# Gathers of selected rows issued one by one over four blocks, with the swap of the choice, two scan steps, the last statistics and a pooling moved in a block loop

## The chip, the cores and the metric

One core of one Trainium2 chip. The metric is the device time of an execution in microseconds (us), with the median of several runs as the kernel's time. Besides, one execution was taken with the hardware profiler; its span, waits and instruction times are what "the profile" and "the trace" mean below. PE is the matmul engine (PEld its weight loads), DVE the vector engine, ACT the scalar (activation) engine, POOL the GpSimd engine, SP the queue that issues most DMAs.

## The reference, cut to what matters

Two layers over `x` of shape (4, 128, 64, 64), that is four samples (b = 0 to 3) of 4096 tokens with 128 channels. All is fp32.

```python
# layer 0: three 1x1 convolutions with PReLU, then attention over all 4096 tokens
score = softmax(einsum('nci,ncj->nij', e1, e2), axis=2)
x = x + einsum('nij,ncj->nci', score, asm)
t = to_tokens(x)                                  # (4, 4096, 128)

# layer 1, attention with a running maximum and running sums over the tokens (8 heads)
kv = silu(einsum('btd,ed->bte', ln(t), W_kv))     # k and v
s = einsum('hd,bthd->bth', q_proj, k)
m = cummax(s, axis=1)
w = cumsum(exp(s - m)[..., None] * v, axis=1)
u = cumsum(exp(s - m), axis=1)
t = t + (w / u[..., None]).mean(axis=2)

# layer 1, experts (64) choose tokens
probs = softmax(ln(t) @ gate_w.T + gate_b, axis=1)   # over the tokens
topv, topi = top_k(probs, 8)                         # 8 tokens for each expert and sample
pooled = einsum('bked,bke->bed', gather(ln(t), topi), topv)
h = gelu(pooled @ weight1); out = h @ weight2        # with bias rows
t = t + scatter_add(topi, out * topv)
```

## The kernel before

Three stages follow each other on the core. Stage one (up to about 1526 us) is layer 0: PE computes scores (`sc`, L1812), ACT their exponentials, PE the weighted sums (`av`, L1837), DVE the row sums. Stage two is a loop over blocks of 512 tokens, 8 blocks for each sample, 32 in all. Stage three is the experts and the final stores.

The block loop is a hand-written schedule: PE, ACT, DVE and POOL take their instructions in the order in which the program records them[...]. `loop` runs over `n` from 6 to 37. In one round it computes the keys of block `n` (`keys`, PE `f_pk`, ACT silu, DVE product and reduction) and values, totals, products and outputs of block `m = n - 6` (`value`: PE `f_pv`, ACT silu into `f_amb`; `totals`: `f_pt`; `products` and `outputs`: `f_po`). "Block m" below is the round of that m.

A round has named places at which other work is put in. `slot(1)` to `slot(4)` each call `point()`, which advances a counter and runs what `later(delay, fn)` has put off to it; then they run what `make_plan` has put at that place of that block with `at(block, place, fn, ...)`. Besides the slots there are "D", "T" and "G", which only run planned work: D after the first products, T after the totals are closed, G at the end of the round behind the outputs. In order of a round: keys 0 and 1, slot 1, values 0 and 1, slot 2, keys 2 and 3, first totals and products, D, slot 3, values 2 and 3, the token transpose `f_ltr` (L965) of block n + 1, slot 4, late totals, `close_totals` (DVE copy L1168), T, `weights(m + 1)` on POOL (L1092 to L1113), late products, `outputs` (PE L1185), `gate_stats`, G.

The running maximum and sum go in groups of four blocks. `keys` puts off `scan0(g)`, which starts a chain: `scan0` (PE transpose `f_str` L1026, DVE copy L1027 and scan L1028), then `scan1` (PE `f_mr` L991 and small DVE steps), `scan2`, `scan2b`, `scan3`, `scan4`. A group's last key stands in slot 2's work of block 4g - 3.

Several small results share one PSUM buffer, tag "sm" with a single copy: `f_str`, `f_mc`, `f_etr`, the gate's logits `f_pl` (L1280), the swap `f_pw` (L1309), `f_pq` and `f_pp` (L1401). Each new one waits until DVE has read the one before it.

The choice of tokens for sample b follows six blocks after the sample's last: `merge_half`, `merge_halves` (the swap: PE `f_pw`, DVE L1310 to L1315), `candidate_rows` (DVE L1321, L1323 makes the row numbers `f_at`), `exps` on ACT, `gathers` (POOL, eight indirect DMAs L1329, each of 128 rows of 512 bytes from the table in HBM into `f_e1b`), `count`, `denominators`, `select` and `pool` (PE `f_pp`, eight products with the gathered rows, DVE copy L1402).

Statistics of layer 1's first normalisation are kept per sample. Those of the last sample (b = 3) are closed in block 6 by `close_stats` (ACT square root L260, DVE L263 and L264):

```python
slot(4)
if m == 6:
    close_stats(B - 1)
```

Of the kernel before, what the change touches and what calls it, by code (L numbers as in the profile page):

```python
# [9 lines left out]
AF = mybir.ActivationFunctionType  # L10
ALU = mybir.AluOpType
# [6 lines left out]
def conv_attn_hybrid_kernel(  # L18
# [24 lines left out]
    nc = tc.nc  # L43
    B, C, N = x.shape
# [19 lines left out]
    eps5 = const.tile([P, 1], F32, tag="eps5", name="eps5")  # L64
# [763 lines left out]
    def fast():  # L828
# [14 lines left out]
        NB = len(blocks)  # L843
# [3 lines left out]
        def later(delay, fn):  # L847
            env.tasks.append((env.now + delay, fn))
# [119 lines left out]
        def keys(n, c):  # L968
            g = n // GB
            s = scan_at(g % 2).rearrange("p (i h) -> p i h", h=NH)  # L970
            pk = ps.tile([P, 2, BLK], F32, tag="kv", name=f"f_pk_{n}_{c}", bufs=2)
            for i in range(2):
                nc.tensor.matmul(  # L973
                    pk[:, i, :], xt_at(n)[:, bass.ts(c, P)], env.wks[:, bass.ts(i, BLK)],
                    start=True, stop=True,
                )
            flat = env.e1a[:, bass.ts(env.ks_count % 2, HD)]
            env.ks_count += 1
            ks = flat.rearrange("p (h c) -> p h c", h=NH)
            nc.scalar.activation(flat, pk.rearrange("p i x -> p (i x)"), AF.Silu)  # L980
            nc.vector.tensor_mul(ks, ks, env.qb)  # L981
            nc.vector.tensor_reduce(s[:, (n % GB) * CPB + c, :], ks, AX.X, ALU.add)  # L982
            if n % GB == GB - 1 and c == CPB - 1:
                later(3, lambda: scan0(g))

        def sm(what, *shape):
            return ps.tile([P, *shape] if shape else [P, P], F32, tag="sm", name=what)
# [35 lines left out]
        def scan0(g):  # L1023
            group[g] = {}
            pt = sm(f"f_str_{g}")
            nc.tensor.transpose(pt, scan_at(g % 2), ident)  # L1026
            nc.vector.tensor_copy(scan_at(SS), pt)  # L1027
            nc.vector.tensor_tensor_scan(  # L1028
                out=scan_at(MM), data0=scan_at(SS), data1=scan_at(SS), op0=ALU.max,
                op1=ALU.max, initial=LOWEST,  # L1030
            )
            later(1, lambda: scan1(g))

        def scan1(g):
            group[g]["m"] = link_rows(g, ends_to_row(g, scan_at(MM), MR, "mr"), 0, ML)
            later(2, lambda: scan2(g))
# [287 lines left out]
                out=at, in0=ci, scalar1=env.base[:, b : b + 1], scalar2=None, op0=ALU.add  # L1324
            )

        def gathers(b):
            for k in range(8):
                nc.gpsimd.indirect_dma_start(  # L1329
                    out=g_at(k), out_offset=None, in_=table[b],  # L1330
                    in_offset=bass.IndirectOffsetOnAxis(ap=sel[b]["at"][:, k : k + 1], axis=0),
                )
# [216 lines left out]
        slots = []  # L1549
# [124 lines left out]
        def layer0(env):  # L1674
            ps, one, big = env.ps, env.one, env.big
            with ExitStack() as l0:
# [286 lines left out]
                keys(LAG, 1)  # L1963
                point()

        plan = {}

        def at(i, slot, fn, *args):
            plan.setdefault((i, slot), []).append((fn, args))
# [5 lines left out]
        def make_plan():  # L1975
            turned = {}
            for lo in range(0, NB - 8, 4):
                at(lo + 4, 4, gate_root, lo, 4)
                at(lo + 5, 1, gate_close, lo, 4)
                for m in range(lo, min(lo + 4, NB - 10)):  # L1980
                    turned[m] = m + 5
            for m, i in turned.items():
                at(i, "D", gate_norm, m)
                at(i + 1, 1, gate_turn, m)
                at(i + 1, 3, gate_logits, m)
            at(NB - 4, "D", gate_root, NB - 8, 4)
            at(NB - 4, 4, gate_close, NB - 8, 4)
            at(NB - 2, "D", gate_root, NB - 4, 2)
            at(NB - 2, 4, gate_close, NB - 4, 2)
            at(NB - 1, 1, gate_root, NB - 2, 1)  # L1990
            at(NB - 1, 1, gate_close, NB - 2, 1)
            last = B - 2
            at(NB - 3, "G", exps, last, 0)
            at(NB - 3, "G", exps, last, 1)
            for m in range(NB - 10, NB - 2):
                i = NB - 5 + (m - NB + 10) // 2
                at(i, "D" if m == NB - 6 else "G", gate_norm, m)
                at(i + 1, 1 + m % 2, gate_turn, m)
                at(i + 1, (2 if i == NB - 2 else 3) + m % 2, gate_logits, m)
            at(NB - 1, 2, gate_norm, NB - 2)  # L2000
            at(NB - 1, 3, gate_turn, NB - 2)
            at(NB - 1, 4, gate_logits, NB - 2)
            for b in range(B - 2):
                i = (b + 1) * NBLK + 6
                at(i - 1, 3, merge_half, b, NBLK)
                at(i, 1, merge_halves, b)
                at(i, 3, candidate_rows, b, NBLK)
                at(i, 4, exps, b, 0)
                at(i, "G", gathers, b)
                at(i + 4, 4, exps, b, 1)  # L2010
                j = i + 5 if b + 3 == B else i + 6
                at(j, 3 if b + 3 < B else 2, count, b)
                at(j + 1, 1, denominators, b)
                at(j + 1, 3 if b + 3 < B else "G", select, b)
                at(j + 1, 4, pool, b)
            at(NB - 4, 4, merge_half, last, NBLK)
            at(NB - 3, 1, merge_halves, last)
            at(NB - 3, 2, candidate_rows, last, NBLK)
            at(NB - 3, "G", gathers, last)
            at(NB - 2, 2, count, last)  # L2020
            at(NB - 2, "G", select, last)
            at(NB - 1, 1, denominators, last)
            at(NB - 1, 4, pool, last)
            at(NB - 1, 4, merge_half, B - 1, NBLK - 1)
            at(NB - 1, "T", merge_halves, B - 1)
            at(NB - 1, "T", candidate_rows, B - 1, NBLK - 1)
            at(NB - 1, "T", gathers, B - 1)

        def loop():
            make_plan()  # L2030
            normals(LAG + 1)
            for n in range(LAG, NB + LAG):
                m = n - LAG

                def slot(p):
                    if n > LAG or p > 1:
                        point()
                    run(m, p)

                if n > LAG and n < NB:  # L2040
                    keys(n, 0)
                    keys(n, 1)
                slot(1)
                if m:
                    weigh_rows(m)
                value(m, 0)
                value(m, 1)
                slot(2)
                if n < NB:
                    keys(n, 2)  # L2050
                    keys(n, 3)
                else:
                    value(m, 2)
                open_block(m)
                totals(0)
                if n < NB:
                    totals(1)
                    products(m, 0)
                run(m, "D")
                if 2 <= m < 6:  # L2060
                    for i in range(CPB):
                        tile_stats(env.rest, B - 1, (m - 2) * NBLK + i)
                slot(3)
                if n < NB:
                    value(m, 2)
                value(m, 3)
                if n + 1 < NB:
                    tokens(n + 1)
                if n + 2 < NB:
                    normals(n + 2)  # L2070
                slot(4)
                if m == 6:
                    close_stats(B - 1)
                if n >= NB:
                    totals(1)
                    products(m, 0)
                totals(2)
                totals(3)
                close_totals(m)
                run(m, "T")  # L2080
                if m + 1 < NB:
                    weights(m + 1)
                for x4 in range(1, CPB):
                    products(m, x4)
                outputs(m)
                gate_stats(m)
                if 2 <= m < 6:
                    for i in range(CPB, 2 * CPB):
                        tile_stats(env.rest, B - 1, (m - 2) * NBLK + i)
                run(m, "G")  # L2090
                if n == NB - 1:
                    for room in (env.wks, env.held[:, bass.ts(2, HD)], slot_of(env.e1a, 0),
                                 slot_of(env.e1a, 1)):
                        load_into(room)
                if n == NB + 2:
                    load_into(slot_of(env.e1a, 2))
                if n == NB + LAG - 2:
                    load_into(slot_of(env.e1a, 3))
            while env.tasks:
                point()  # L2100
            assert not plan, plan.keys()
# [99 lines left out]
```

## Time and profile before

| | us |
|---|---|
| median of 3 runs | 2364.94 |
| lowest, highest | 2362.34, 2367.75 |
| the profiled execution, whole | 2383.13 |
| its span | 2381.1 |
| busy in the span: PE, DVE, ACT, POOL | 2271.9, 1450.8, 1095.0, 180.2 |
| PE's mean granted clock | 0.989 |

The profile was taken in another execution than the timed runs. Each part of a page is read by itself: the first gives an engine's busy time, the 40 slices show where in the span it is spent, the list of waits names who waited for whom with total, count and longest in us, and a timeline line has the start, the duration, engine, source line, operation, output and inputs, and in brackets the engine's idle time before it with what ended it. The block loop is the slices 26 to 38 of the 40:

```profile
PE   7999999999999999999999999999999999899877
PEclk9999999999999999999999999999999999999799
DMA  2000010000010000010000000102111112134394
```

### The profile page before, as it was taken

How to read it: one execution, taken by the hardware profiler on the slowest of the kernel's cores; microseconds unless marked ns; L12 is line 12 of the kernel's file. 1: busy time of each engine (PE TensorE's matmuls, PEld its weight loads, DVE VectorE, ACT ScalarE, POOL GpSimd, SP SyncE). 2: the span in 40 equal slices, each digit the busy share in tenths (PEclk: the TensorE clock that was granted, in tenths of full speed). 3: DMA queues.
4: the chain of work that ended last, by engine and by line, in shares of the span. 5: the costliest groups of instructions: out<-in, count | busy, mean ns of one | idle time of the engine just before them, and what ended most of it. 6: DMA issues, size and time to landing. Idle time of an engine off the chain costs nothing.

```text
span 2381.1 us, 43376 instructions
## 1 busy us (share of the span) xinstructions
PE 2271.9 (95%) x18530; PEld 1189.0 (50%) x18530; DVE 1450.8 (61%) x2345; ACT 1095.0 (46%) x1329; POOL 180.2 (8%) x340
## 2 busy tenths in 40 slices
PE   7999999999999999999999999999999999899877
PEld 3544444444444444444444444555555556566554
DVE  7666566556566556556555566577676668665414
ACT  2343333433333433334444544455565566456531
POOL 0000000000000000000000000112112221223200
PEclk9999999999999999999999999999999999999799
DMA  2000010000010000010000000102111112134394
GB/s 86 20 12 16 9 44 16 9 8 16 9 43 17 8 8 16 9 35 12 9 5 5 5 5 5 50 26 58 45 39 59 48 49 56 33 114 107 134 344 189
DMA packets 72587, 105.82 MB, mean 44 GB/s; under 512 B 8512, under 2 KB 44352, under 8 KB 72384
## 3 DMA queue, kind: packets, MB, share of 16 engines
q1 hardware_dynamic: 70784, 99.81, 13.4%
q8 instruction: 147, 2.41, 0.4%
q0 software_dynamic: 1024, 2.10, 0.3%
q10 hardware_dynamic: 576, 1.05, 0.1%
q14 instruction: 56, 0.46, 0.1%
HBM read 79.60 MB, written 17.04 MB: 41 GB/s over the span
## 4 chain that ended last, share of the span: by engine, by line
PE 86%; DVE 6%; ACT 4%; issue 2%; DMA 1%; another core or an unknown queue 1%; POOL 0%; SPq 0%; ACTq 0%; DVEq 0%; POOLq 0%
PE av L1837 36%; PE sc L1812 18%; PE f_pv L1128 9%; PE f_pk L973 7%; PE f_pt L1151 3%; PE f_po L1174 2%; PE pd L1863 1%; ACT f_e1a L980 1%; PE pa L1785 1%; DVE f_e1a L981 1%; PE pe L1759 1%; DVE f_e1a L982 1%; PE f_po L1185 1%; PE f_eo L1625 1%; PE f_pl L1280 1%
## 5 line engine op out<-in xcount | busy, mean ns | idle before, releaser
L1837 PE MATMUL av<-pr,am 64*128 64x512 f32 x4096 | 976.3, 591 | 1.7 <-ACT pr L1817 1.7
L1817 ACT ACTIVATE pr<-sc 128x1024 f32<-128x1024 f32 x512 | 523.6, 1023 | 779.7 <-PE sc L1812 766.8
L1824 DVE TENSOR_TENSOR acc<-acc,pr 128x1024 f32<-128x1024 f32 x480 | 586.6, 1222 | 483.9 <-ACT pr L1817 479.6
L1837 PEld LDWEIGHTS av<-pr,am 64*128 64x128 f32 x4096 | 401.3, 187 | 471.0 <-issue 457.8
L1812 PE MATMUL sc<-e,e 64*128 64x512 f32 x2048 | 534.5, 591 | 4.8 <-DMA e<-side 4.8
L1812 PEld LDWEIGHTS sc<-e,e 64*128 64x128 f32 x2048 | 201.3, 187 | 236.3 <-issue 228.6
L1128 PE MATMUL f_pv<-f_held,f_ama 128*32 128x256 f32 x4096 | 244.7, 385 | 7.7 <-ACT f_e1a L980 4.0
L973 PE MATMUL f_pk<-f_held,f_ama 128*128 128x512 f32 x512 | 240.7, 615 | 9.0 <-ACT f_amb L1133 8.5
L1133 ACT ACTIVATE f_amb<-f_pv 128x1024 f32<-128x1024 f32 x128 | 130.8, 1023 | 157.1 <-PE f_pv L1128 136.6
L981 DVE TENSOR_TENSOR f_e1a<-f_e1a,f_held 128x1024 f32<-128x1024 f32 x128 | 156.2, 1221 | 68.6 <-ACT f_e1a L980 68.3
L980 ACT ACTIVATE f_e1a<-f_pk 128x1024 f32<-128x1024 f32 x128 | 129.9, 1024 | 126.3 <-PE f_pk L973 62.6
L1128 PEld LDWEIGHTS f_pv<-f_held,f_ama 128*32 128x32 f32 x4096 | 131.5, 111 | 105.9 <-issue 20.4
L982 DVE TENSOR_REDUCE f_e1a<-f_e1a 128x8 f32<-128x1024 f32 x128 | 155.3, 1218 | 3.5
L973 PEld LDWEIGHTS f_pk<-f_held,f_ama 128*128 128x128 f32 x512 | 94.1, 193 | 122.0 <-issue 103.1
L1092 POOL COPY f_held<-f_e1a 32x32 f32<-32x32 f32 x128 | 30.3, 237 | 944.7 <-DVE f_e1a L1074 564.2
L1151 PE MATMUL f_pt<-f_amb,f_held 128*32 128x128 f32 x1920 | 83.7, 277 | 1.2 <-ACT f_amb L1133 1.2
L918 POOL MEMSET f_held<- 128x1024 f32 x1 | 1.0, 956 | 1034.8 <-DVE xn L1750 1034.8
L1151 PEld LDWEIGHTS f_pt<-f_amb,f_held 128*32 128x32 f32 x1920 | 60.2, 109 | 11.0 <-issue 5.1
L1190 DVE TENSOR_TENSOR t<-t,f_po 128x512 f32<-128x512 f32 x32 | 22.0, 687 | 56.4 <-PE f_po L1185 56.4
L956 ACT ACTIVATE f_xl<-t,ln_nb,ln_rs 128x128 f32<-128x128 f32 x128 | 52.8, 491 | 0.8 <-PE pa L1785 0.8
L1261 ACT ACTIVATE f_x<-t,f_gnb,f_grs 128x128 f32<-128x128 f32 x126 | 51.3, 482 | 0.4 <-DVE f_gnb L1242 0.4
L1821 DVE COPY acc<-pr 128x1024 f32<-128x1024 f32 x32 | 22.2, 693 | 39.3 <-ACT pr L1817 39.3
(265 smaller groups left out, 1829.2 us busy)
## 6 DMA issues: line engine op xcount, KB each, us to landing
f_e2a<-f_rd SPq DMA_DIRECT2D x128, 128.0 KB
xr<-in_xtok_dram SPq DMA_DIRECT2D x32, 256.0 KB
out_dram<-t SPq DMA_DIRECT2D x16, 512.0 KB
f_table<-f_x SPq DMA_DIRECT2D x62, 128.0 KB
f_held<-in_fw_dram SPq DMA_DIRECT2D x14, 512.0 KB
f_e1a<-in_fw_dram SPq DMA_DIRECT2D x13, 512.0 KB
x<-in_x_dram SPq DMA_DIRECT2D x12, 512.0 KB
f_amb<-in_fw_dram SPq DMA_DIRECT2D x12, 512.0 KB
```

The source lines that it names most:

```text
L956: nc.scalar.activation(xl[:, c, :], t[:, b * NCH + i, :], AF.Identity, bias=ln_nb[:, b, i : i + 1], scale=ln_rs[:, b, i : i + 1],)
L973: nc.tensor.matmul(pk[:, i, :], xt_at(n)[:, bass.ts(c, P)], env.wks[:, bass.ts(i, BLK)], start=True, stop=True,)
L980: nc.scalar.activation(flat, pk.rearrange("p i x -> p (i x)"), AF.Silu)
L981: nc.vector.tensor_mul(ks, ks, env.qb)
L982: nc.vector.tensor_reduce(s[:, (n % GB) * CPB + c, :], ks, AX.X, ALU.add)
L1128: nc.tensor.matmul(pv[a * CH : (a + 1) * CH, i, :], xt_at(m)[:, bass.ts(c * NA + i, CH)], env.wvs[:, bass.ts(a, HH * C)], start=True, stop ...
L1133: nc.scalar.activation(env.amb[:, bass.ts(c, HD)], pv.rearrange("p i x -> p (i x)"), AF.Silu)
L1151: nc.tensor.matmul(env.pt[i * CH : (i + 1) * CH, :], lhs, rhs, start=i not in env.begun, stop=False, skip_group_check=True,)
L1812: nc.tensor.matmul(sc[:, u, :], e2[halves[u], p, :], e1[halves[u], cols], start=True, stop=True,)
L1817: nc.scalar.activation(pr, sc, AF.Exp)
L1824: nc.vector.tensor_add(acc, acc, pr)
L1837: nc.tensor.matmul(av, am[h, j, :], pr[h, u, :], start=(j == 0), stop=(j == NCH - 1))
```

## The change

Six edits, all in where work is put; what is computed stays the same.

- `scan0` is put off by two points and not three, and `scan1` by two and not one, so that `scan0` runs at slot 4 of blocks 1, 5, 9 and so on and not at slot 1 of the next block, and `scan1` where it ran.
- `merge_halves` of samples 0 and 1 goes from slot 1 to slot 2.
- `gathers` takes a range of its eight DMAs. For samples 0 and 1 they are put one by one at G of block i, then slot 3 and G of the following blocks up to slot 3 of i + 4 (i = 14 and 22). For sample 2 they are put at eight places from slot 3 of block 29 to slot 1 of block 31, where all had been at G of block 29. Sample 3's stay together.
- `pool` of sample 0 goes from slot 4 to G of block 21.
- `close_stats` of the last sample is split: the square root on ACT stays at slot 4 of block 6 (`last_root`), the two DVE operations are put at slot 1 of block 7 (`last_close`).

```diff
@@ keys
             if n % GB == GB - 1 and c == CPB - 1:
-                later(3, lambda: scan0(g))
+                later(2, lambda: scan0(g))
@@ scan0
-            later(1, lambda: scan1(g))
+            later(2, lambda: scan1(g))
@@
-        def gathers(b):
-            for k in range(8):
+        def gathers(b, lo, hi):
+            for k in range(lo, hi):
                 nc.gpsimd.indirect_dma_start(
                     out=g_at(k), out_offset=None, in_=table[b],
                     in_offset=bass.IndirectOffsetOnAxis(ap=sel[b]["at"][:, k : k + 1], axis=0),
@@
+        def last_root():
+            nc.scalar.activation(
+                ln_rs[:, B - 1], ln_mv[:, B - 1, :, 1:2].rearrange("p i o -> p (i o)"), AF.Sqrt,
+                bias=eps5,
+            )
+
+        def last_close():
+            b = B - 1
+            nc.vector.reciprocal(ln_rs[:, b], ln_rs[:, b])
+            nc.vector.scalar_tensor_tensor(
+                out=ln_nb[:, b], in0=ln_mv[:, b, :, 0:1].rearrange("p i o -> p (i o)"),
+                scalar=-1.0, in1=ln_rs[:, b], op0=ALU.mult, op1=ALU.mult,
+            )
@@ make_plan
+            at(7, 1, last_close)
@@ make_plan, for b in range(B - 2): i = (b + 1) * NBLK + 6
-                at(i, 1, merge_halves, b)
+                at(i, 2, merge_halves, b)
                 at(i, 3, candidate_rows, b, NBLK)
                 at(i, 4, exps, b, 0)
-                at(i, "G", gathers, b)
+                for k in range(8):
+                    at(i + (k + 1) // 2, 3 if k % 2 else "G", gathers, b, k, k + 1)
@@
-                at(j + 1, 4, pool, b)
+                at(j + 1, "G" if b + 3 < B else 4, pool, b)
@@
-            at(NB - 3, "G", gathers, last)
+            slots = [(NB - 3, 3), (NB - 3, 4), (NB - 3, "G"), (NB - 2, 1), (NB - 2, 3),
+                     (NB - 2, 4), (NB - 2, "G"), (NB - 1, 1)]
+            for k, (i, place) in enumerate(slots):
+                at(i, place, gathers, last, k, k + 1)
@@
-            at(NB - 1, "T", gathers, B - 1)
+            at(NB - 1, "T", gathers, B - 1, 0, 8)
@@ loop
                 if m == 6:
-                    close_stats(B - 1)
+                    last_root()
```

## The prediction

> **What bounds the kernel now.** I read the page's slices first, then PE's waits and the windows of the block loop (1526 to 2250 us), then the timeline round each wait.
>
> ```profile
> PE 2271.9 (95%) x18530; PEld 1189.0 (50%) x18530; DVE 1450.8 (61%) x2345; ACT 1095.0 (46%) x1329; POOL 180.2 (8%) x340
> ```
>
> PE carries the span (86% of the chain that ended last), so an edit counts only where it removes a stretch in which PE stands still or runs slowly. In stage one nothing does. In the loop these four do:
>
> ```profile
> PE f_pk L973 <- ACT f_amb L1133: 8.5, 2, 4.6
> PE f_pw L1309 <- DVE f_e1a L1027: 8.0, 2, 4.0
> PE f_mr L991 <- DVE f_e1a L1028: 5.1, 4, 1.9
> PE f_po L1185 <- POOL f_e1b L1113: 4.0, 1, 4.0
> ```
>
> ```profile
> 1700.00:1750.00 50.00, 49.71 (x797) 30.12 (x786) 32.88 (x59) 30.38 (x47) 12.42 (x24) 1.00 0.22 63
> 1850.00:1900.00 50.00, 44.97 (x660) 26.51 (x656) 31.61 (x58) 27.40 (x41) 16.58 (x24) 0.97 0.16 40
> 2050.00:2100.00 50.00, 45.21 (x664) 25.99 (x660) 32.69 (x55) 27.95 (x42) 17.57 (x24) 0.97 0.19 52
> ```
>
> A clean window has PE busy 49.7 of 50 us at clock 1.00; the two with gathers lose 5 us and some clock. Block lengths show the same: from one token transpose (L965) to the next a block takes 21.9 us (blocks 9, 13, 17), but 23.8 in block 6, 28.9 in 7, 27.9 in 14, 29.0 in 15, 29.4 in 22 and 29.2 in 23.
>
> The swap of block 14:
>
> ```profile
> 1840.19 0.27 PE L1026 MATMUL f_str<-ident,f_e1a 128*128 128x128 f32 x1
> 1843.42 1.22 DVE L982 TENSOR_REDUCE f_e1a<-f_e1a 128x8 f32<-128x1024 f32 x1
> 1844.56 0.28 DVE L1027 COPY f_e1a<-f_str 128x128 f32<-128x128 f32 x1
> 1844.89 0.39 PE L1309 MATMUL f_pw<-f_both,f_swap 128*128 128x8 f32 x2 [4.00 <-DVE f_e1a L1027]
> ```
>
> f_str and f_pw share the one "sm" buffer in PSUM; L1027 empties it, but stands on DVE behind two keys' products (4 x 1.22 us).
>
> The last statistics, in block 6:
>
> ```profile
> 1677.80 0.32 ACT L260 ACTIVATE ln_rs<-ln_mv,eps 128x32 f32<-128x32 f32 x1
> 1678.15 0.35 DVE L263 RECIPROCAL ln_rs<-ln_rs 128x32 f32<-128x32 f32 x1 [4.89 <-ACT ln_rs L260]
> 1678.64 0.28 DVE L1168 COPY f_e1b<-f_pt 128x128 f32<-128x128 f32 x1
> 1679.03 1.94 PE L1185 MATMUL f_po<-f_e1b,f_ama 128*32 128x128 f32 x32 [4.04 <-POOL f_e1b L1113]
> ```
>
> The page blames POOL, but the wait ends only after L1168, which stood behind L263, which waited 4.89 us for ACT's table loads. The gathers, in block 14's tail:
>
> ```profile
> 1867.27 1.16 POOL L1329 DMA_INDIRECT f_e1b<-f_table,f_at  x1 [0.17 <-DVE f_gmv L1227]
> 1876.57 0.94 POOL L1329 DMA_INDIRECT f_e1b<-f_table,f_at  x1 [0.30 <-issue]
> 1878.88 1.02 ACT L1133 ACTIVATE f_amb<-f_pv 128x1024 f32<-128x1024 f32 x1 [5.58 <-remote]
> 1879.96 1.22 PE L973 MATMUL f_pk<-f_held,f_ama 128*128 128x512 f32 x1 [4.62 <-ACT f_amb L1133]
> ```
>
> ACT waits for PE's semaphore alone. PE began that value's last matmul at 1872.96, yet the semaphore came at 1878.86, with the eighth gather's landing. So a burst of eight holds back what PE posts.
>
> [...] half-clock records of 3.413 us after each wait above, 6.83 us after the statistics (an f_pk pass 1222 for 592 ns). [...] here the last gather's semaphore was complete 2.4 us after its issue. [...]
>
> **The change, part by part.** The reference is the profiled execution, 2383.13 us (span 2381.1).
>
> *First scan step one point earlier, second at its old point.* f_str now stands before the late totals of blocks 1, 5, 9 ... 25, its copy L1027 and scan L1028 before L1168. Does PE wait for f_str's input? The last L982 of those blocks ends 1.76 us (blocks 1, 5), 2.48 (9, 13, 17) and 1.14 (21) before PE gets there: no. Does L1168 come later? DVE idles 2.69 us before it in block 13; 0.28 + 0.42 us fit. If that cover were gone: 0.7 us in seven blocks, about 5. Removed: f_mr's waits, 1.30 + 1.86 + 0.96 + 0.96 = **5.1 us**. Group 0's step moves within stage one, where DVE has idle time before 480 additions: nothing.
>
> *Swap to slot 2.* "sm" has been empty for most of a block by then, so f_pw waits for nothing. Block 14 falls from 27.9 to 21.9: 4.0 of wait and 2.0 of half clock and restart. Next in line are the kv buffers, free since 1841.5, and L1122, which still ends 3 us before products need it. Twice 6.0 = **12.0 us**. DVE's four small operations (0.6 us) only change places.
>
> *Statistics.* ACT's root stays, the two DVE operations go to block 7's slot 1 (0.35 + 0.19 us before L1122, whose product PE takes 2 us after its end, 1693.4 to 1695.5: hidden). Late next: ACT's loads. PE would do L1185 at 1675.0, keys to 1679.8, the transpose to 1680.4; ACT, done at 1678.1, loads the silu table (1.28) and frees the first kv buffer at about 1680.5. Values start at 1680.6 and not 1687.1: 6.5, by block length 28.9 - 22.0 = **6.9 us**.
>
> *Gathers.* Not one at a time on the queue: between a "G" and the next slot 3 POOL has nothing else and waits for nothing, so they issue in pairs, four for sample 0 and four for sample 1; for sample 2 two, four and two go together. Each group but sample 2's first stands right behind a block's weights. New: the weights' copy L1092 waits for a pair's landing, with L1094, L1099 and L1113 behind it and L1122 on DVE after those. A pair has landed 1.25 + 2.4 = 3.7 us after its first issue; L1092 comes some 20 us later, except in block 29, where the first pair can go only after L1323 (2185.0) and lands at about 2188.8, just when L1092 starts (2188.90): below 0.5 us, and L1122 has 1 us to spare. The burst's price by block length: 29.0 - 22.0 = 7.1, 29.2 - 22.0 = 7.2, and in block 29 7.2 (the gate's product L1280 begins at 2206.1; after the transpose's end at 2195.7 one value of 1.83 us and 1.3 us of totals put it at 2198.9): 21.5 in all. The fourth burst stays. What does a pair cost? The trace has none. Below: nothing, as in the burst's first 3.5 us PE posted on time; above: 3.7 us each. I take 1.5 us for all of them, since the pairs end before the hold showed.
>
> *Pooling of sample 0 behind the outputs.* Same 16 matmuls (1.9 us); between no gain and 1.0 (L1168 of block 21 starts that late): I take 0.
>
> **Sum.** The waits give 24.0 us, certain in kind. The hold may belong to the profiled execution in part: that is 18.2 us longer than the median 2364.94, and the holds (21.5 + some 4.8 in the fourth burst, DVE 3.01 and PE 1.82 with no releaser, = 26.3) are the only stretches I cannot lay to an instruction. If the excess is all hold, 26.3 - 18.2 = 8.1, about a third, is left in plain runs: 6.6 of the 21.5. So 2364.9 - 24.0 - 6.6 + 1.5 = **2336 us**. In the profile: 2383.1 - 24.0 - 21.5 + 1.5 = 2339.
>
> **Rivals.**
> - *The hold is real in every run.* For it: the semaphores are the program's own. Against: the 18.2 us. 2364.9 - 24.0 - 21.5 + 1.5 = 2321.
> - *The scan gives back what it took:* L1027 and L1028 delay L1168, and the gathers bring nothing. Against: the idle 2.69 us. 2364.9 - 24.0 + 5.3 = 2346.
> - *Slower: each group holds PE as the burst did.* Eleven groups, ten of 3.7 us and one of 6.2, and 1.7 us of half clock after each: 37 + 6.2 + 18.7 = 62 in place of 21.5, so 2364.9 - 24.0 + 40 = 2381. It decides from 46 us of holds on, which needs a hold that starts with a group's first gather. Against: f_pv's first half in block 15 was posted at 1872.26, with four gathers already through.
> - *No change*: the waits turn into others at once. DVE, busy 33 of 50 us, speaks against.
>
> **Chances.** Forecast 0.57 (own range 2328 to 2344), real hold 0.24, give-back 0.10, slower 0.06, none 0.03. The range 2316 to 2349 leaves out the last two and the edges. A measurement of this kernel tells no change from 0.2%, 4.7 us: faster 0.91, same 0.03, slower 0.06.
>
> **What would show it.** After: no f_pw or f_mr wait on DVE; blocks 6, 7, 10, 14, 18 near 22 us; L1168 of block 6 right behind its totals; gathers in pairs; no ACT wait on "remote" before the last choice. Wrong would be: PE waiting at f_str for L982, L1185 waiting for L1168 in blocks 1 to 25, remote waits behind each pair, or a median above 2350 with all waits gone.

## The result, and the profile after

| | before | after |
|---|---|---|
| median, us | 2364.86 | 2340.21 |
| lowest to highest, 5 runs each | 2362.34 to 2367.75 | 2337.43 to 2343.35 |
| profiled execution (its span) | 2383.13 (2381.1) | 2340.21 (2338.3) |

The ratio is 0.9897, 95% interval 0.9883 to 0.9912: 24.65 us less. The forecast was 2336 (range 2316 to 2349) for plain runs and 2339 for the profiled execution.

The page after, busy times:

```profile
PE 2259.9 (97%) x18530; PEld 1187.3 (51%) x18530; DVE 1452.7 (62%) x2345; ACT 1095.1 (47%) x1329; POOL 183.5 (8%) x340
```

PE has 12.0 us less busy time for the same 18530 matmuls. The half-clock records (stretches with a granted clock of 0.5) between 1526 us and the last choice, 23.9 us in six before, are down to one of 3.4 us. The list of PE's waits in the block loop and the end of it (1520 to 2270 us; total, count, longest), costliest first:

```profile
PE f_otr L1567 <- ACT t L1568: 6.1, 9, 0.7
PE f_pv L1128 <- ACT f_e1a L980: 4.6, 12, 0.7
PE f_eo L1625 <- DVE f_e1b L1621: 4.5, 9, 0.6
PE f_gtr L1273 <- ACT f_x L1261: 2.4, 1, 2.4
```

The four that headed the list before (f_pk 8.5, f_pw 8.0, f_mr 5.1, f_po 4.0) are gone, and no single wait here is longer than 2.4 us, that of f_gtr, which was there before as well (2.4, 1, 2.4). f_otr and f_eo belong to stage three, which now starts 43 us earlier and so fills more of this fixed window; no wait has moved to them. The two windows with gathers that were shown before, after the change (first PE's busy time, then weight loads, DVE, ACT, POOL, PE's clock, DMA share, GB/s):

```profile
1850.00:1900.00 50.00, 49.41 (x741) 28.86 (x739) 35.62 (x62) 32.85 (x46) 16.82 (x24) 1.00 0.20 59
2050.00:2100.00 50.00, 49.40 (x772) 29.47 (x774) 34.05 (x58) 28.68 (x38) 17.57 (x24) 1.00 0.43 124
```

PE was busy 44.97 and 45.21 us in them; now they are nearly as full as the clean one was (49.71). The swap of block 14, on the timeline of after:

```profile
1834.71 0.39 PE L1309 MATMUL f_pw<-f_both,f_swap 128*128 128x8 f32 x2
1836.86 0.15 DVE L1310 COPY f_both<-f_pw 128x8 f32<-128x8 f32 x1
```

f_pw waits for nothing; DVE, which was late before, reads it only 2 us later, and PE has gone on by then. The last statistics in blocks 6 and 7:

```profile
1671.81 0.29 DVE L1168 COPY f_e1b<-f_pt 128x128 f32<-128x128 f32 x1 [0.48 <-PE f_pt L1151]
1672.71 0.27 PE L1185 MATMUL f_po<-f_e1b,f_ama 128*32 128x128 f32 x1
...
1675.86 0.32 ACT L1967 ACTIVATE ln_rs<-ln_mv,eps 128x32 f32<-128x32 f32 x1
1676.20 1.28 ACT L980 ACT_TABLE_LOAD   x1
1678.58 3.66 PE L1128 MATMUL f_pv<-f_held,f_ama 128*32 128x256 f32 x64 [0.58 <-ACT f_e1a L980]
...
1683.67 0.33 DVE L1974 RECIPROCAL ln_rs<-ln_rs 128x32 f32<-128x32 f32 x1
1684.03 0.19 DVE L1975 SCALAR_TENSOR_TENSOR ln_nb<-ln_mv,ln_rs 128x32 f32<-128x32 f32 x1
```

L1168 no longer stands behind the reciprocal. What is late next is ACT, as forecast: after the root it loads the silu table again (1.28 us), and PE's values wait 0.58 us for it. The first two gathers, which go as a pair in block 14's tail, with the two activations (ACT L1133) that a burst had held before:

```profile
1851.51 1.16 POOL L1329 DMA_INDIRECT f_e1b<-f_table,f_at  x1 [0.17 <-DVE f_gmv L1227]
1852.98 0.95 POOL L1329 DMA_INDIRECT f_e1b<-f_table,f_at  x1 [0.30 <-issue]
1855.34 1.03 ACT L1133 ACTIVATE f_amb<-f_pv 128x1024 f32<-128x1024 f32 x1 [0.66 <-PE f_pv L1128]
1857.06 1.02 ACT L1133 ACTIVATE f_amb<-f_pv 128x1024 f32<-128x1024 f32 x1 [0.70 <-PE f_pv L1128]
```

Neither activation waits on "remote", the profile's word for a wait whose end it can lay to no instruction. Block lengths of both traces, here from the end of one block's last L1185 to the end of the next block's:

| block | before | after | what went |
|---|---|---|---|
| 2, 10, 18 | 22.26, 23.07, 23.07 | 20.67, 21.83, 21.83 | f_mr's waits |
| 6 and 7 | 29.07 + 24.18 | 21.83 + 22.66 | statistics, one f_mr wait |
| 14 | 28.01 | 22.05 | f_pw's wait |
| 21 and 22 | 23.41 + 28.01 | 22.44 + 23.84 | f_pw's wait; sample 0's pooling (1.9 us) now counts in 22 |
| 15, 23, 30 | 29.44, 29.62, 23.52 | 22.39, 22.38, 15.83 | the hold of the burst |
| 28 | 18.50 | 20.16 | a half-clock record of 3.41 us, from 2134.1 |

Blocks 1 to 31 are 44.9 us shorter in the profile. Blocks 15, 23 and 30 make 21.98 of that; the other 22.9 (24.6 without block 28) come close to the 24.65 that plain runs gained. So the two profiles differ by the hold of the bursts as well, and the plain runs seem not to. Why was the hold not in them?

### The profile page after: what moved, and what is told of

Same layout as the page of the kernel before. It is cut to its first block, busy times and chain, and to the rows that moved or that the text cites. A ratio compares the mean times of both kernels' runs of the same rounds, so it can differ in the third digit from the quotient of the medians.

```text
span 2338.3 us, 43371 instructions
## 1 busy us (share of the span) xinstructions
PE 2259.9 (97%) x18530; PEld 1187.3 (51%) x18530; DVE 1452.7 (62%) x2345; ACT 1095.1 (47%) x1329; POOL 183.5 (8%) x340
## 4 chain that ended last, share of the span: by engine, by line
PE 89%; DVE 5%; ACT 3%; DMA 2%; issue 1%; POOL 0%; SPq 0%; ACTq 0%; DVEq 0%; POOLq 0%
PE av L1837 37%; PE sc L1812 18%; PE f_pv L1128 9%; PE f_pk L973 8%; PE f_pt L1151 3%; PE f_po L1174 2%; PE pd L1863 1%; PE pa L1785 1%; PE pe L1759 1%; PE f_po L1185 1%; ACT f_e1a L980 1%; PE f_eo L1625 1%; DMA x<-in_x_dram 1%; PE f_ph L1588 1%; PE f_eo L1615 1%
## 5 line engine op out<-in xcount | busy, mean ns | idle before, releaser
L1128 PE MATMUL f_pv<-f_held,f_ama 128*32 128x256 f32 x4096 | 237.8, 381 | 5.3 <-ACT f_e1a L980 4.6
L973 PE MATMUL f_pk<-f_held,f_ama 128*128 128x512 f32 x512 | 234.9, 603 | 0.0
L1133 ACT ACTIVATE f_amb<-f_pv 128x1024 f32<-128x1024 f32 x128 | 130.7, 1023 | 125.0 <-PE f_pv L1128 125.0
L1261 ACT ACTIVATE f_x<-t,f_gnb,f_grs 128x128 f32<-128x128 f32 x126 | 51.3, 482 | 0.4 <-DVE f_gnb L1242 0.4
```

Source lines behind the costliest of these rows:

```text
L973: nc.tensor.matmul(pk[:, i, :], xt_at(n)[:, bass.ts(c, P)], env.wks[:, bass.ts(i, BLK)], start=True, stop=True,)
L1128: nc.tensor.matmul(pv[a * CH : (a + 1) * CH, i, :], xt_at(m)[:, bass.ts(c * NA + i, CH)], env.wvs[:, bass.ts(a, HH * C)], start=True, stop ...
L1133: nc.scalar.activation(env.amb[:, bass.ts(c, HD)], pv.rearrange("p i x -> p (i x)"), AF.Silu)
```

## The experiments

Three groups of kernels ran, each on one chip with the kernel before beside it. The chips are called A, B and C here:

| chip | kernel before: median (lowest to highest, runs) |
|---|---|
| A | 2366.09 (2362.90 to 2369.84, 19) |
| B | 2389.25 (2382.78 to 2394.51, 11) |
| C | 2365.68 (2363.59 to 2368.31, 17) |

The same kernel is 23.2 us slower on B than on A, without overlap. This was not known when the expectations for A and B were written, which take 2365 or 2366 as the kernel before.

### The gathers alone, and everything but the gathers (chip A)

The kernel before with only the gathers spread (`...` stands for lines left out here: the range arguments of `gathers` and the list `slots`, both as in the change):

```diff
-                at(i, "G", gathers, b)
+                for k in range(8):
+                    at(i + (k + 1) // 2, 3 if k % 2 else "G", gathers, b, k, k + 1)
...
-            at(NB - 3, "G", gathers, last)
...
+            for k, (i, place) in enumerate(slots):
+                at(i, place, gathers, last, k, k + 1)
```

> The kernel before with the gathers of samples 0 to 2 spread, and nothing else of the change. Theory (the hold of the gather bursts belongs to the one profiled execution of the kernel before and is not there in plain runs): no change, 2365 us (2362 to 2367). Rival 1 (the hold is real in every run, 21.5 us): 2343 to 2347. Rival 2 (a third of it is real, as the prediction took it: 6.6 less 1.5 for the groups): 2360.

Measured: 2366.41 against 2366.09, ratio 1.0001 (0.9993 to 1.0010). No change.

The kernel after with the bursts put back:

```diff
-                for k in range(8):
-                    at(i + (k + 1) // 2, 3 if k % 2 else "G", gathers, b, k, k + 1)
+                at(i, "G", gathers, b, 0, 8)
...
-            for k, (i, place) in enumerate(slots):
-                at(i, place, gathers, last, k, k + 1)
+            at(NB - 3, "G", gathers, last, 0, 8)
```

> The kernel after with the gathers of samples 0 to 2 in bursts of eight behind the gate, as before. Theory (no hold in plain runs): same as the kernel after, 2340 us (2338 to 2343); whether its profiled execution shows ScalarE waits on remote behind the eighth gather is open. Rival 1 (hold real): 2340 + 21.5 - 1.5 = 2360. Rival 2 (a third): 2345.

Measured: 2340.98, ratio 0.9897 (0.9881 to 0.9912), the same as the kernel after (2340.21). The burst in block 14's tail of this kernel, first, fifth and eighth gather and the two activations that were held before:

```profile
1852.26 1.16 POOL L1329 DMA_INDIRECT f_e1b<-f_table,f_at  x1 [0.17 <-DVE f_gmv L1227]
...
1856.08 1.03 ACT L1133 ACTIVATE f_amb<-f_pv 128x1024 f32<-128x1024 f32 x1 [0.66 <-PE f_pv L1128]
...
1857.65 0.94 POOL L1329 DMA_INDIRECT f_e1b<-f_table,f_at  x1 [0.30 <-issue]
1857.81 1.02 ACT L1133 ACTIVATE f_amb<-f_pv 128x1024 f32<-128x1024 f32 x1 [0.70 <-PE f_pv L1128]
...
1861.56 1.28 POOL L1329 DMA_INDIRECT f_e1b<-f_table,f_at  x1 [0.30 <-issue]
```

Eight gathers 1.25 to 1.46 us apart, as before, and in their midst ACT goes on as soon as PE's matmuls end: it idles 0.7 us each time. On chip A a burst holds nothing, profile or not, so spreading it is worth nothing there.

### Scan and swap together, and the statistics alone (chip A)

The first is the kernel before with these lines, the pooling's among them:

```diff
-                later(3, lambda: scan0(g))
+                later(2, lambda: scan0(g))
...
-            later(1, lambda: scan1(g))
+            later(2, lambda: scan1(g))
...
-                at(i, 1, merge_halves, b)
+                at(i, 2, merge_halves, b)
...
-                at(j + 1, 4, pool, b)
+                at(j + 1, "G" if b + 3 < B else 4, pool, b)
```

> The kernel before with the scan's two steps and the swap moved, and sample 0's pooling behind the outputs; gathers and last statistics as before. Theory (the waits add up): 2364.9 - 5.1 - 12.0 = 2348 us. Rival (the scan gives back what it took because its copy and scan delay the last totals, 0.7 us in seven blocks): 2353. If the moved steps do nothing in plain runs: 2365.

Measured: 2348.26, 17.8 less, ratio 0.9918 (0.9904 to 0.9931). The prediction's two terms give 17.1.

The second has the statistics' edit alone (`last_root` and `last_close` as in the change):

```diff
-                    close_stats(B - 1)
+                    last_root()
...
+            at(7, 1, last_close)
```

> The kernel before with the last statistics alone split between block 6 and block 7. Theory: block 6 falls by the 6.9 us of its wait and restart, 2358 us. Rival (values then wait for ScalarE's table loads in place of that, and only the VectorE wait of 4.0 us without its half clock goes): 2361. If the new place of the two VectorE operations delays block 7's products: 2363 or more.

Measured: 2359.52, 6.6 less, ratio 0.9975 (0.9964 to 0.9987). In its trace block 6 falls from 29.07 to 23.96 (an f_mr wait stays in it) and block 7 from 24.18 to 22.66: together 6.6. The two gains, 17.8 and 6.6, make 24.4 of the 24.65.

### Scan alone and swap alone (chip B)

The first has only the two `later` lines above, the second only the `merge_halves` line.

> The kernel before with the first scan step one point earlier and the second at its old point, nothing else. The prediction's split (the scan owns only the f_mr waits, the swap owns the two f_pw waits): 2366.1 - 5.1 = 2361 us. Rival (f_str leaves the shared PSUM buffer a point earlier, so this edit alone also takes away both f_pw waits and their half clock): 2366.1 - 17.1 = 2349. If copy and scan delay the last totals by 0.7 us in seven blocks: 5 us more than either.

Measured: 2372.68 against 2389.25: 16.6 less, ratio 0.9932 (0.9916 to 0.9948), the rival's 17 and not the split's 5.

> The kernel before with the swap of each of samples 0 to 2 at slot 2 in place of slot 1, nothing else. Prediction's step: the two waits of f_pw go with their half clock, 2 x 6.0: 2366.1 - 12.0 = 2354 us. Rival (the wait passes to the next user of the buffer or to f_pk, so that only part comes back): 2358 to 2366. Third user: sample 0's block 7 swap loses another 1.0 to 1.5 if it stood in a wait too: 2353.

Measured: 2379.20, 10.0 less, ratio 0.9958 (0.9942 to 0.9973), between the 12.0 of the prediction's step and the rival's 8 at most. (The expectation speaks of samples 0 to 2; the line moves the swap of samples 0 and 1.)

16.6 and 10.0 together are more than the 17.8 of both edits on chip A: the two edits remove the same wait. Block 13 and 14 of the kernel with the scan's edit alone, where f_pw still stands at slot 1:

```profile
1830.33 0.27 PE L1026 MATMUL f_str<-ident,f_e1a 128*128 128x128 f32 x1
1830.63 0.29 DVE L1027 COPY f_e1a<-f_str 128x128 f32<-128x128 f32 x1 [1.58 <-PE f_str L1026]
1831.74 0.29 DVE L1168 COPY f_e1b<-f_pt 128x128 f32<-128x128 f32 x1 [0.35 <-PE f_pt L1151]
...
1837.77 0.29 PE L1309 MATMUL f_pw<-f_both,f_swap 128*128 128x8 f32 x2
```

The copy that empties the shared PSUM buffer now runs in block 13, before L1168, which still waits for PE and not for DVE: nothing is given back there. Seven us later f_pw finds the buffer free; blocks 14 and 22 are 21.95 each. Something is lost in block 21 instead (25.86 us, before 23.41), where sample 0's pooling (f_pp), still at slot 4, now meets the same late copy:

```profile
2014.16 2.00 PE L1401 MATMUL f_pp<-f_e2b,f_e1b 128*128 128x64 f32 x16 [2.07 <-DVE f_e1a L1027]
```

With the swap alone blocks 14 and 22 are 23.3, since f_str keeps its late place and f_mr now stops PE there too, as its list of waits shows (before: 5.1, 4, 1.9):

```profile
PE f_mr L991 <- DVE f_e1a L1028: 7.0, 6, 1.9
```

Chip B also showed what had been missing on A. The eight gathers of block 14's tail in the trace of the scan's edit alone (first, fifth and eighth shown):

```profile
1858.35 1.16 POOL L1329 DMA_INDIRECT f_e1b<-f_table,f_at  x1 [0.17 <-DVE f_gmv L1227]
...
1860.18 4.36 PE L1128 MATMUL f_pv<-f_held,f_ama 128*32 128x256 f32 x64 [0.30 <-ACT f_e1a L980]
...
1863.76 0.94 POOL L1329 DMA_INDIRECT f_e1b<-f_table,f_at  x1 [0.30 <-issue]
1863.99 1.02 ACT L1133 ACTIVATE f_amb<-f_pv 128x1024 f32<-128x1024 f32 x1 [2.47 <-remote]
...
1867.66 0.94 POOL L1329 DMA_INDIRECT f_e1b<-f_table,f_at  x1 [0.30 <-issue]
1869.83 1.02 ACT L1133 ACTIVATE f_amb<-f_pv 128x1024 f32<-128x1024 f32 x1 [4.82 <-remote]
1870.91 2.07 PE L973 MATMUL f_pk<-f_held,f_ama 128*128 128x512 f32 x2 [3.86 <-ACT f_amb L1133]
```

POOL issues at the same pace as on A. PE's matmuls for the second activation end at 1864.54, but ACT starts it only at 1869.83, 2.2 us after the start of the eighth gather. Six such waits make 21.8 us (21.8 in this trace, 22.0 with the swap alone), and block 15 is 29.21 and 29.20. The kernel before takes 23.2 us more on B, and its fastest run there is 12.9 slower than its slowest on A, so on B the hold must be in the plain runs too.

### The pooling put back, and PE kept busy in the last choice (chip B)

The kernel after with sample 0's pooling ahead of the late totals of block 21 again:

```diff
-                at(j + 1, "G" if b + 3 < B else 4, pool, b)
+                at(j + 1, 4, pool, b)
```

> The kernel after with sample 0's 16 pooling matmuls back ahead of the last totals of block 21. The prediction took their move as nothing. Theory from the two traces (blocks 21 and 22 together fall by 5.1 us in the kernel after against 6.0 in block 14, so the move costs 0.8 to 0.9, since the matmuls had covered the end of L1168): 2339.4 us, 0.9 less than the kernel after. Rival (nothing): 2340.3. Other rival (the late totals of block 21 now get the scan's copy ahead of them, and the matmuls save up to 1.0): 2341.

Measured: 2344.30 on chip B, where the kernel before takes 2389.25: ratio 0.9813 (0.9797 to 0.9828), 45 us less. The six long waits are gone from its trace. Spreading the gathers by itself was not run on B; that it is what takes the hold away there rests on this kernel and the next, which have spread gathers, beside the two above, which have bursts. The expectation, 0.9 us less than the kernel after, missed: the pooling's old place costs time. That was read from the trace (below) and timed again on chip C.

The last sample's choice has 2.4 us in which PE waits for f_x (ACT L1261), and a half-clock record of 23.9 us, which starts inside that wait at 2195.6 us. The next kernel is the kernel after with these waits filled with transposes that are due there anyway, some done twice (the choice of the buffer in `turn_early`, adapted to this, is left out):

```diff
-            turn_early(0)
-            turn_early(1)
+            for n in (0, 1, 2, 3, 2, 3):
+                turn_early(n)
             gate_turn(m)
-            turn_early(2)
+            turn_early(3)
             gate_logits(m)
+            turn_early(2)
             turn_early(3)
...
             nc.tensor.matmul(pw, env.swap, late, start=True, stop=True)
+            for n in (2, 3, 2):
+                turn_early(n)
```

> The kernel after with the early transposes of the last choice moved ahead of the gate's and some of them done again (same values), so that PE has no long stand between 2193.8 and 2202.7 us of the profile. Theory (the half-clock record of 23.9 us from 2195.6 follows from the 2.4 us wait on f_x, and the 18 us of matmuls under it take twice as long): up to 9 us less, 2331 to 2335. Rival (the choice is a chain through VectorE and ScalarE, and PE's clock does not set its length, or short waits bring the half clock back): 2339 to 2341. Slower if the repeated transposes stand ahead of awaited matmuls: over 2341.

Measured: 2345.03, ratio 0.9815 (0.9799 to 0.9832), no gain over the 2344.30 beside it. Since that one loses over 4 us by its pooling, and this one does not, the transposes seem to have cost about as much; the expectation of up to 9 us less fell. The trace shows why, with PE, DVE and POOL in the last choice:

```profile
2200.12 0.36 PE L1454 MATMUL f_pw<-f_e1b,f_swap 128*128 128x8 f32 x2 [0.52 <-issue]
2200.34 1.51 PE L1425 MATMUL f_etb<-ident,t 128*128 128x128 f32 x12
2202.09 0.94 POOL L1329 DMA_INDIRECT f_e1b<-f_table,f_at  x1 [0.30 <-issue]
2203.97 0.17 DVE L1460 COPY f_merged<-f_pw 128x8 f32<-128x8 f32 x1 [3.79 <-remote]
```

f_pw was done at 2200.5; DVE saw it 3.5 us later, 1.9 us after the start of the eighth gather of sample 3. In the kernel with the pooling back, on the same chip with the same eight gathers, nothing follows f_pw on PE for 1.8 us, and DVE reads it 0.04 us after its end. From the end of the last L1185 to the first L1588 the choice takes 21.27 us here and 18.21 there.

### After again, the gathers alone again, the pooling, and PE kept busy once more (chip C)

Two kernels are repeated as they were, the pooling is put beside the kernel after, and the last is the previous one without the transposes behind f_pw. This chip turned out to be like A, so what the first two expectations say of a chip like B stays untested.

> The kernel after, unchanged, once more beside before. The two chips so far differ: on one the kernel before takes 2366 us and its gather bursts hold nothing, on the other 2389 us with the holds in every profile. Theory (the hold is a matter of the chip, and the change takes it away where it is): on a chip where before takes 2366, this takes 2341 (24.7 less); where before takes 2389, this takes 2389.3 - 24 - 21.5 + 1.5 = 2345 or less (some 45 less). Rival (the waits alone give the gain everywhere, and the slow chip is slow all over): 2364 where before takes 2389.

Measured: 2340.42, ratio 0.9895 (0.9880 to 0.9910): 25.3 less.

> The kernel before with the gathers of samples 0 to 2 spread, once more. Theory: where before takes 2366, the same as before; where before takes 2389, about 21.5 - 1.5 = 20 less, 2369. Rival (spread gathers hold PE as the burst does): 2389 or more on the slow chip.

Measured: 2365.38 against 2365.68, ratio 0.9998 (0.9990 to 1.0007). No change, as on A.

> The kernel after with sample 0's pooling back ahead of the last totals of block 21, once more, now beside the kernel after on the same chip. Its first profile shows block 21 at 29.10 us against 22.44, and block 22 at 22.05 against 23.84: the pooling's product needs the PSUM buffer of f_str, 2.06 us until L1027 empties it, and half clock for 6.83 us. Theory: 4.9 us slower than the kernel after, plus or minus 1.5. Rival (nothing, as the prediction took the move of the pooling): same as the kernel after.

Measured: 2344.73, against 2340.42 of the kernel after beside it: 4.3 more, with single runs that touch (2342.17 to 2345.76 and 2339.00 to 2343.66). The traces show where the time goes. Block 21 with the pooling back:

```profile
1998.34 0.27 PE L1026 MATMUL f_str<-ident,f_e1a 128*128 128x128 f32 x1
2000.22 0.22 DVE L1303 MAX8 f_both<-f_e1b 128x8 f32<-128x64 f32 x1
2000.36 0.27 DVE L1027 COPY f_e1a<-f_str 128x128 f32<-128x128 f32 x1
2000.69 3.21 PE L1401 MATMUL f_pp<-f_e2b,f_e1b 128*128 128x64 f32 x16 [2.07 <-DVE f_e1a L1027]
```

and in the kernel after on the same chip:

```profile
2000.34 0.27 PE L1026 MATMUL f_str<-ident,f_e1a 128*128 128x128 f32 x1
2002.36 0.27 DVE L1027 COPY f_e1a<-f_str 128x128 f32<-128x128 f32 x1
2003.01 0.26 DVE L1168 COPY f_e1b<-f_pt 128x128 f32<-128x128 f32 x1
2003.38 1.08 PE L1185 MATMUL f_po<-f_e1b 128*32 128x128 f32 x32 [0.37 <-issue]
2004.39 2.00 PE L1401 MATMUL f_pp<-f_e2b,f_e1b 128*128 128x64 f32 x16
```

f_pp too uses the buffer of f_str, which L1027 empties late in this block, behind DVE's selection. Back at slot 4 PE stands 2.07 us for it and then runs 6.83 us at half clock (f_pp takes 3.21 for 2.00). Blocks 21 and 22 together: 29.11 + 22.05 = 51.16 against 22.44 + 23.83 = 46.27, 4.9 us.

The same kernel takes 2344.73 on C and 2344.30 on B: with the gathers spread the chip hardly matters, with bursts it does (the kernel before: 2365.68 and 2389.25). Something is left on B, though. Where four gathers of sample 2 go together in block 30, DVE waits on "remote" there too:

```profile
2167.48 0.65 PE L1280 MATMUL f_pl<-f_e1b,f_gws 128*64 128x256 f32 x4
2168.44 0.94 POOL L1329 DMA_INDIRECT f_e1b<-f_table,f_at  x1 [0.30 <-issue]
2170.17 0.48 DVE L1284 TENSOR_SCALAR f_lg<-f_pl,f_gbs 128x256 f32<-128x256 f32 x1 [2.81 <-remote]
```

f_pl ends at 2168.13 and DVE starts 2.0 us later; on C it does not idle at this place. Before that, in block 29, the pair of sample 2 makes ACT's L1133 idle for 2.00 us on B and 0.98 on C. The kernel with the filled waits shows the same on B (2.92 on DVE, 2.01 on ACT).

> The kernel after with the early transposes of the last choice ahead of the gate's, some done again with the same values, but none behind f_pw (there they held f_pw's semaphore for 3.8 us in the first try). Theory (the half clock from the wait on f_x is what costs): 2 to 6 us less than the kernel after. Rival (the chain through VectorE and ScalarE sets the choice's length): same as the kernel after within 1 us.

Measured: 2339.74, ratio 0.9888 (0.9872 to 0.9903), 0.7 less than the kernel after: the same within the spread. Its half-clock record starts at 2202.8 us and is 17.1 long, that of the kernel after on this chip at 2199.0 and is 20.5 long, yet f_pc is only 0.2 us nearer to f_pw (2.18 us from start to start for 2.38), and the choice takes 17.76 us for 18.19. Between the two, PE waits for 1.82 us in both traces, for small steps of DVE and ACT that follow one another. No version tried beat the kernel after by more than its runs spread.

## Why the prediction was right

**The sum of the waits** was right: 24.0 was forecast, 24.65, 25.1 (with bursts) and 25.3 were measured on chips without the hold. Its terms were each less exact. By the block lengths, f_mr's waits gave 6.2 for 5.1, f_pw's 11.1 for 12.0 (with the pooling's cost in it) and the statistics 6.6 for 6.9, so part of the agreement is luck.

**Scan and swap.** The total, 17.1, was right (17.8). The split into 5.1 and 12.0 was not: the step gave f_pw's wait to the swap, because the swap was the edit that moves f_pw. The wait was for L1027, and the scan's edit moves that one; alone it is worth 16.6. That f_str costs nothing at its new place was right: blocks 1, 5, 9, 13, 17 and 25 are as long as before, and the rival in which the scan gives back 5.3 fell.

**Statistics.** 6.9 was forecast, 6.6 measured; ACT's silu table was what was late next.

**Pooling of sample 0.** "I take 0" was right only as a balance. The working named the shared buffer for f_str and f_pw and left out f_pp, which had not followed f_str closely before. Without its move the scan's edit makes PE wait 2.07 us in block 21. That makes block 21 2.45 us longer in the trace of the scan's edit alone, and it costs 4.9 with the half clock in the kernel with the pooling back. Against the kernel before, the two blocks come out at 5.14 us less where block 14 alone gains 5.96: 0.8 us of cost in place of 0.

**The hold: the mis-sized term.** The step took "about a third" of 21.5 us as left in plain runs, 6.6, with 1.5 for the pairs. It read one number, the 18.2 us by which the profiled execution exceeded the median, as a fraction. On A and C the hold is zero and the pairs cost nothing (the gathers alone: ratios 1.0001 and 0.9998), and the result's own chip, which isn't listed, takes 2364.86 us as they do. So these 5.1 us, less the 0.65 that the waits gave beyond 24.0, are the forecast's miss of a little over 4. On B the hold is whole: 23.2 us in the kernel before. The median stayed inside the range because the term was small, not because it was right. The premise of the fraction was wrong as well. The fourth burst was counted with 4.8 us of hold, but from the end of the last L1185 to the first L1588 both traces take 18.8 us, and the trace of after has the same idle times of DVE (3.01) and PE (1.82): no hold. The excess of 18.2 was then close to the other three bursts' 21.5, which pointed to all or nothing. The 2339 for the profiled execution (2340.21 measured) takes the whole hold off a time that had the whole hold in it, and so needed no fraction.

That the profile of before was taken on a chip like B is inferred, for its chip isn't listed: it has the waits on "remote", its 2383.13 us lie inside B's range and outside those of A and C, and like the traces of B it gives the gathers no landing time (last section). The profile of after gives one, like those of A and three of C. The kernel after itself was not run on B; that it would be some 49 us faster there (2389.25 less about 2340) follows only from the kernel with the pooling back, which takes the same time on B and C.

**Rivals.** The real hold (2321) mixed the time of one kind of chip with the holds of the other. "Slower" needed a long hold from each group. On A and C no trace shows one. On B the groups of sample 2 do hold, the pair by 1 us and the four by 2, and blocks 29 and 30 are 15.48 and 16.77 against 14.93 and 16.03 on C: 1.3 us in all, near the 1.5 that was taken. The reading against this rival was wrong: f_pv's first half in block 15, posted at 1872.26, had ended at 1871.03, so it was 1.2 us late already, with four gathers issued.

## What to carry to other kernels

When a profiled execution lies outside the range of the timed runs, first ask whether it ran on the same chip; a stretch that no instruction explains may then be wholly present on one chip and wholly absent on another, as here (21.8 us of such waits on B, none in the burst's trace on A), and not a fraction. For a buffer with one copy, list every tile that uses it in the order in which PE reaches them, and credit a wait to the edit that moves the instruction which empties it. An edit that looks free may be what keeps another edit's gain.

## What the runs showed of the hardware

- On B, in the midst of a burst of eight indirect DMAs, ACT started 5.3 us after the end of PE's matmuls that it waits for (1864.54 to 1869.83 above). On A it idled 0.66 and 0.70 us at the same two places, with the same pace on POOL: the eighth gather starts 9.31 us after the first on B and 9.30 on A. For C this rests on times alone: 2365.68 with bursts and 2365.38 without.
- The records of the gathers differ too. Neither the profile of before nor the four of B give the gathers a landing time. The profile of after does (median 2.8 us from issue to landing), and so do the four of A (2.5 to 2.8) and three of C (2.6 to 2.9). In the trace of before the semaphores of the first burst's eight gathers have 8, 4, 3, 4, 5, 5, 4 and 16 updates by DMA, in that of after 31 of the 32 gathers have 16 and one has 13. Whether records are missing or updates came otherwise, and what differs in the chip, is not settled.
- On B a burst does not hold every post. In the last choice f_pw's was seen 3.5 us late when twelve transposes followed it and 0.04 us after its end when PE stood idle, but with the pooling back f_gtr (end 2201.66, read at 2201.69) and f_pl (2203.24, read at 2203.28) were on time with other matmuls right behind them. What else the hold needs is open.
- How much half clock goes with a stall varies. In the profile of before both waits of f_pw (4.0 us each) were followed by a half-clock record of 3.41 us (block 14: 28.01 us), while the wait of 4.04 us at the statistics has one of 6.83 (block 6: 29.07), which starts 0.8 us before the wait ends. A stall of 2.06 or 2.07 us was followed by 6.83 us at half clock in both traces with the pooling back, and by none in the trace of the scan's edit alone (f_pp takes 2.00 us there, 3.22 and 3.21 in the others). None follows f_mr's waits of up to 1.9 us either, though the prediction has a record after each wait that it lists. What sets the length of a record is not shown.
